# Decoder layer on one core: maxima sent to their row by transfers, softmax sums inverted on sixteen partitions, layer-norm roots in fewer operations

## The chip, the cores and the metric

The kernel runs on one NeuronCore of a Trainium2 chip. The core has a matrix engine (TensorE, PE in the profile; its weight loads are shown as PEld), a vector engine (VectorE, DVE), an engine for activation functions (ScalarE, ACT), a general engine (GpSimd, POOL) and an engine that issues transfers (SyncE, SP). Each works through its own list of instructions in a fixed order and waits on semaphores for the others. Sixteen DMA engines move data between the memory on the chip (SBUF, 128 partitions) and HBM, or from SBUF to SBUF. Matmul results land in PSUM.

The metric is the device time of one execution in microseconds. The kernel before takes 5403.67 us (median of 3 runs, 5400.97 to 5409.85).

## What is computed

A decoder layer in float32 on x of shape (8, 512, 512): a state-space block (Mamba), cross-attention to a context of the same shape, and a mixture of 32 experts, each with a residual and a layer norm. Cut to what matters here:

```
def _layernorm(x, axis=-1, eps=1e-05):
    m = jnp.mean(x, axis=axis, keepdims=True)
    v = jnp.var(x, axis=axis, keepdims=True)
    return (x - m) / jnp.sqrt(v + eps)
...
    scores = jnp.einsum('bnlh,bnph->bnlp', qm, km) / np.sqrt(HEAD_DIM).astype(np.float32)
    mask = attention_mask[:, None, None, :]
    scores = jnp.where(mask, scores, MASK_FILL)
    attn = jax.nn.softmax(scores, axis=-1)
    out = jnp.einsum('bnlp,bnph->bnlh', attn, vm)
...
    x = _layernorm(x + _L0_attn_ref(x, ...), axis=-1)
    x = _layernorm(x + _L0_xattn_ref(x, ctx_1024, ctx_1024, mask_BxS2_bf1, ...), axis=-1)
    x = _layernorm(x + _L0_ffn_ref(x, ...), axis=-1)
```

There are 16 heads of 32 dimensions, 512 queries and 512 keys in each of 8 batches.

## The kernel before, in words

`layers` handles the Mamba block, the attention and the routing; `experts` the 32 experts; `finish` the last layer norm.

The scan goes through 16 chunks (8 batches of two chunks of 256 positions). A chunk has 32 steps. In each step DVE does three large operations: the input product (L494), the scan itself (L501) and the product with C (L510); ACT makes the decays for the next step (L480); PE folds the result of two steps together (L521). Their inputs are copies of dt and dtx, four times repeated over partitions, which SP fetches with transfers (`repeat`, L428), and of B and C, which go to HBM and come back spread over the partitions (`x_proj` L408, `bcast` L418).

The attention of batch b-1 is cut into small parts by `units`, and these are laid between the steps of batch b's two chunks: a list of parts with weights, taken as the running sum allows. The attention of the last batch has no scan to lie under and runs after it. A part returns a follow-up that is put into the program a little later; `wait` puts it three thirds of a step later, and outside the scan it has no effect. The order in which each engine's instructions finally stand is fixed by the framework's scheduler when the program is built.

The parts that the change touches, for a pair of heads i (8 pairs a batch):

- `spread` (L793) brings the pair's q and k to the tiles `qa` and `ka`, 64 partitions a head: 32 rows of data, and then rows that add the mask and the negative maximum to the scores within the same matmul. The row of `qa` that will hold the maximum is first set to zero; the row of `ka` against it holds ones (L269 to L274).
- `maximum` (L805) runs four times, for 128 queries each: two matmuls (L813) with queries on the output partitions, and one DVE reduction (L815) to one value for each query and head.
- `negate` (L817) turns the 128x2 maxima into rows by four PE transposes (L822), ACT multiplies by -1 (L826), and two transfers (L829) put the rows into `qa`.
- `weigh` (L833): the matmuls the other way round (L839), keys on the partitions, and the exponential on ACT (L843).
- `gather` (L847): the product with v (L855). v has 32 columns of ones beside it, so that 32 rows of the result hold the softmax's sum. ACT copies the result to SBUF (L867), and four transfers move the products to `attT` (L875) and the sums, 32 equal rows a head, to `total` (L876).
- `divide` (L880), for two pairs of heads at a time (4 a batch, 32 in all): `total` is 128 partitions by 512 queries. Its reciprocal comes from ACT (Ln and Exp, L888 and L889) and a Newton step on DVE, and the same operations scale `attT` (L892 to L894).
- `output` (L902) is the matmul with Wo (L750), which needs all four parts of `attT`.

`layernorm` (L54) runs 40 times: ln1 and ln2 on 2 tiles in each of 16 chunks, ln3 on 4 tiles in each of 8 batches. Besides the statistics it has a DVE operation that adds EPS (L64), Ln and Exp on ACT (L68, L69) and four DVE operations (L73 to L76) that improve the root by a Newton step.

Of the kernel before, what the change touches and what calls it, by code (L numbers as in the profile page):

```python
# [17 lines left out]
P = 128  # L18
B, S, D = 8, 512, 512
DC = D // P  # L20
# [30 lines left out]
ROW = D + E + 1  # L51


def layernorm(nc, pool, tiles, outs, name, wait=lambda part: part, then=None):  # L54


    n = len(tiles)
    mv = pool.tile([P, n, 2], F32, tag=f"{name}mv")
    for j, t in enumerate(tiles):
        st = pool.tile([P, 6], F32, tag=f"{name}st")  # L60
        nc.vector.bn_stats(st, t)
        nc.vector.bn_aggr(mv[:, j, :], st)
    v = pool.tile([P, n], F32, tag=f"{name}v")
    nc.vector.tensor_scalar(v, mv[:, :, 1], EPS, None, ALU.add)  # L64

    def roots():
        r = pool.tile([P, n], F32, tag=f"{name}r")
        nc.scalar.activation(r, v, AF.Ln)  # L68
        nc.scalar.activation(r, r, AF.Exp, scale=-0.5)  # L69

        def scaled():
            m = pool.tile([P, n], F32, tag=f"{name}m")
            nc.vector.tensor_tensor(m, v, r, ALU.mult)  # L73
            nc.vector.tensor_tensor(m, m, r, ALU.mult)
            nc.vector.tensor_scalar(m, m, -0.5, 1.5, ALU.mult, ALU.add)
            nc.vector.tensor_tensor(r, r, m, ALU.mult)  # L76
            less = pool.tile([P, n], F32, tag=f"{name}less")
            nc.vector.scalar_tensor_tensor(less, mv[:, :, 0], -1.0, r, ALU.mult, ALU.mult)
            for j, (t, o) in enumerate(zip(tiles, outs)):
                nc.scalar.activation(o, t, AF.Identity, bias=less[:, j : j + 1], scale=r[:, j : j + 1])  # L80
            if then:
                then()

        return wait(scaled)

    return wait(roots)


def layers(ctx, tc, a, x1d, filld, based, xbuf):
# [38 lines left out]

    ident = cp.tile([P, P], F32, name="l_ident")
    make_identity(nc, ident)  # L130

    def const(name, shape, src):
        t = cp.tile(shape, F32, name=f"l_{name}")
# [66 lines left out]

    ones = cp.tile([P, P], F32, name="l_ones")
    nc.gpsimd.memset(ones, 1.0)
    fold = cp.tile([P, QP], F32, name="l_fold")
    for at, sign in ((0, 1), (NQ - 1, -1)):
        nc.gpsimd.affine_select(
# [57 lines left out]
    def later_constants():  # L263

        nc.sync.dma_start(
            aneg.rearrange("p c j g -> p (c j) g"),
            a["A_log"].rearrange("(b c) (s g) -> (c s) b g", c=QP, s=NQ),
        )
        for i in range(NPB):  # L269
            for r0 in (HD + 1, 2 * HD + HD + 1):  # L270
                nc.sync.dma_start(
                    kas[i][r0 : r0 + 1, :].rearrange("p (c t) -> p c t", c=DC),
                    ones[0:1, :].unsqueeze(1).to_broadcast([1, DC, P]),
                )  # L274
# [39 lines left out]
    def norm_x(f):  # L314
        xt = f["xt"]
        xs = [xt[:, j, :] for j in range(NT_)]
        return layernorm(nc, sm, xs, xs, "ln1", wait)

    def flip_x(q, f):
        if q == 0:  # L320
# [221 lines left out]
    def back(half, b, t, f):  # L542
# [15 lines left out]
        def norm():  # L558
            outs = [o[:, j, :] for j in range(NT_)]
            for j in range(NT_):  # L560
                nc.vector.scalar_tensor_tensor(outs[j], pos[j], rs, outs[j], ALU.mult, ALU.add)  # L561
            r0 = b * S + t * T
            to = x1d[r0 : r0 + T, :].rearrange("(j p) d -> p j d", p=P)
            return layernorm(nc, sm, outs, outs, "ln2", wait, lambda: nc.sync.dma_start(to, o))

        return wait(norm)

# [185 lines left out]
    def units(b):  # L753
# [51 lines left out]
        def maximum(i, lt):  # L805

            qa, ka = st[i]
            if lt == 0:
                st["mx", i] = p2.tile([P, SC, 2], F32, tag="mx", name="mx")
            ps = pss.tile([P, 2, S], F32, tag="sc", name="ps_s")  # L810
            for j in range(2):
                r = slice(j * 2 * HD, (j + 1) * 2 * HD)
                nc.tensor.matmul(ps[:, j, :], qa[r, lt * P : (lt + 1) * P], ka[r, :], start=True, stop=True)  # L813
            mx = st["mx", i]
            return lambda: nc.vector.tensor_reduce(mx[:, lt, :].unsqueeze(2), ps, AX.X, ALU.max) and None  # L815

        def negate(i):  # L817

            mx = st.pop(("mx", i))
            pm = psm.tile([P, S], F32, tag="mm", name="ps_m")  # L820
            for lt in range(SC):
                nc.tensor.transpose(pm[0:2, lt * P : (lt + 1) * P], mx[:, lt, :], ident)  # L822
# [24 lines left out]
        def gather(i, kc):  # L847
# [17 lines left out]
            def split():  # L865
                raw = p3.tile([P, D], F32, tag="row", name="raw")
                nc.scalar.copy(raw, po)  # L867
                if i % 2 == 0:
                    st["total"] = p1.tile([P, S], F32, tag="total", name="total")
                attT, total, oc = st["attT"], st["total"], i // 2  # L870
                for j in range(2):

                    r0, r1 = (0, HD) if j == 0 else (3 * HD, 2 * HD)
                    to = slice((i % 2) * 2 * HD + j * HD, (i % 2) * 2 * HD + (j + 1) * HD)
                    nc.sync.dma_start(attT[to, oc, :], raw[r0 : r0 + HD, :])  # L875
                    nc.sync.dma_start(total[to, :], raw[r1 : r1 + HD, :])  # L876

            return split

        def divide(oc):  # L880

            attT, total = st["attT"], st["total"]

            late = wait if oc < DC - 1 else lambda part: part

            def inverse():
                r = p3.tile([P, D], F32, tag="row", name="r")
                nc.scalar.activation(r, total, AF.Ln)  # L888
                nc.scalar.activation(r, r, AF.Exp, scale=-1.0)  # L889

                def newton():
                    nc.vector.tensor_tensor(total, total, r, ALU.mult)  # L892
                    nc.vector.scalar_tensor_tensor(total, total, -2.0, r, ALU.add, ALU.mult)
                    nc.vector.scalar_tensor_tensor(  # L894
                        attT[:, oc, :], attT[:, oc, :], -1.0, total, ALU.mult, ALU.mult
                    )

                return late(newton)

            return late(inverse)  # L900

        def output(lt):  # L902
# [9 lines left out]
            def add_up():  # L912
                nc.vector.tensor_tensor(xr, pp, xr, ALU.add)
                nc.vector.tensor_tensor(st["x2"][lt], xr, bo, ALU.add)
                if lt == SC - 1:
                    return layernorm(nc, sm, st["x2"], st["x2"], "ln3")

            return add_up

# [644 lines left out]
```

## Time and profile before

| | us |
|---|---|
| median of 3 runs | 5403.67 |
| the profiled execution's own time | 5406.28 |
| its span, first to last instruction | 5404.6 |
| busy in the span: PE | 4672.4 |
| DVE | 4235.9 |
| ACT | 2593.6 |
| POOL | 570.3 |
| scan with attention of batches 0 to 6 | about 503 to 3522 |
| attention of batch 7 and what follows it up to the experts | about 3522 to 3850 |
| experts | about 3850 to 5340 |

The granted TensorE clock was 0.935 over the span. In a list of groups, a line gives the source line, the engine, the operation, the tiles (out<-in), shapes and count, then the busy time in us and the mean of one in ns, and then the idle time just before these instructions and what ended it. In a list of waits: who waited for whom, total us, times, longest. In a timeline: start, duration, engine and line; in brackets the idle time before it and its releaser. A letter q after an engine's name means its sequencer; SPq lines are issues of transfers, not their duration.

### The profile page before, as it was taken

To read this page: it belongs to the slowest core of one execution; us is meant where nothing else is said; L and a number is where in the kernel's file an instruction comes from. 1 tells how busy PE (TensorE), PEld (TensorE's weight loads), DVE (VectorE), ACT (ScalarE), POOL (GpSimd) and SP (SyncE) were. 2 spreads that over 40 slices of the span, in tenths; PEclk is the share of its full clock that TensorE was granted. 3 is DMA by queue.
4 is the path that set the end of the run, shared out by engine and by line. 5 is a ranking of instruction groups with operands and counts; after the bars stand their busy time and mean duration, and the time that the engine had idled before them with its cause. 6 is when DMAs were issued, how large, how long until landed. Compare 5 with 4: busy or idle time off the path is not lost. (4 is left out here: it accounts for less than half of the span.)

```text
span 5404.6 us, 53991 instructions
## 1 busy us (share of the span) xinstructions
PE 4672.4 (86%) x17320; PEld 2476.6 (46%) x17320; DVE 4235.9 (78%) x5369; ACT 2593.6 (48%) x5726; POOL 570.3 (11%) x426
## 2 busy tenths in 40 slices
PE   6768889788888988988888888789999999999994
PEld 3324234234333423433333342333677777777773
DVE  7999899989989989898998998943566555665554
ACT  5566565565656556566565655523222222222223
POOL 1000002002000200200200020011111111111111
PEclk8879989999999999999999999899999999999997
DMA  8875346345444634634544463342344444544544
GB/s 236 266 224 146 87 96 208 81 114 176 114 104 117 197 77 109 189 98 107 174 125 100 117 200 78 91 146 66 103 128 127 123 117 118 127 127 121 129 115 144
DMA packets 486427, 719.03 MB, mean 133 GB/s; under 512 B 117137, under 2 KB 200625, under 8 KB 484096
## 3 DMA queue, kind: packets, MB, share of 16 engines
q1 hardware_dynamic: 450128, 627.16, 41.1%
q0 software_dynamic: 33280, 76.90, 7.5%
q10 hardware_dynamic: 2736, 11.54, 0.5%
q8 instruction: 137, 2.24, 0.2%
q14 instruction: 146, 1.20, 0.1%
HBM read 391.24 MB, written 165.05 MB: 103 GB/s over the span
## 5 line engine op out<-in xcount | busy, mean ns | idle before, releaser
L480 ACT ACTIVATE l_da<-rep,l_aneg 128x256 f32<-128x256 f32 x2048 | 895.0, 501 | 941.8 <-DVE h L501 877.0
L501 DVE TENSOR_TENSOR_SCAN h<-l_da,h 128x1028 f32<-128x1028 f32 x512 | 1166.0, 2292 | 20.3 <-ACT l_da L480 17.7
L494 DVE TENSOR_TENSOR h<-rep,bc 128x1024 f32<-128x1024 f32 x512 | 614.7, 1218 | 103.1 <-PE py L521 84.6
L510 DVE TENSOR_TENSOR h<-h,bc 128x1024 f32<-128x1024 f32 x512 | 619.5, 1217 | 2.1
L521 PE MATMUL py<-h,l_fold 128*32 128x512 f32 x2048 | 368.3, 644 | 113.4 <-DVE h L510 96.5
L813 PE MATMUL ps_s<-l_ka,l_qa 64*128 64x512 f32 x1024 | 325.6, 707 | 137.8 <-DVE mx L815 137.6
L1314 PE MATMUL ps_h<-xT,w 128*128 128x320 f32 x1536 | 435.8, 433 | 0.0
L1394 POOL DMA_INDIRECT based<-y,xe x160 | 255.5, 1597 | 1309.9 <-ACT y L1417 630.0
L1335 DVE TENSOR_TENSOR hT<-ps_h,p 128x320 f32<-128x320 f32 x128 | 62.9, 492 | 378.5 <-PE ps_h L1314 378.5
L815 DVE TENSOR_REDUCE mx<-ps_s 128x2 f32<-128x1024 f32 x256 | 310.2, 1217 | 58.5 <-PE ps_s L813 58.3
L1314 PEld LDWEIGHTS ps_h<-xT,w 128*128 128x128 f32 x1536 | 292.5, 191 | 118.3 <-issue 0.4
L855 PE MATMUL po<-eT,l_va 128*64 128x512 f32 x1024 | 301.5, 670 | 47.6 <-ACT eT L843 43.1
L839 PE MATMUL ps_t<-l_qa,l_ka 64*128 64x512 f32 x1024 | 308.4, 674 | 23.8 <-ACT eT L843 23.1
L843 ACT ACTIVATE eT<-ps_t 128x1024 f32<-128x1024 f32 x256 | 259.0, 1015 | 128.8 <-PE ps_t L839 128.5
L688 POOL DMA_INDIRECT xbuf<-x2t,dest x128 | 217.2, 1697 | 860.4 <-DVE dest L679 760.8
L1314 PE MATMUL ps_h<-t,s 128*128 128x320 f32 x1024 | 286.1, 432 | 0.0
L343 PE MATMUL ps_z<-xnT,wm 128*128 128x256 f32 x1024 | 238.0, 388 | 30.0 <-DVE o L561 24.3
L750 PE MATMUL ps_p<-x2T,wa 128*128 128x512 f32 x512 | 241.5, 626 | 18.1 <-ACT hT L944 10.4
L552 PE MATMUL po<-wm,zs 128*128 128x512 f32 x512 | 244.7, 632 | 13.8 <-DVE z L957 11.9
L343 PE MATMUL ps_x<-xnT,wm 128*128 128x256 f32 x1024 | 246.5, 393 | 4.5 <-ACT xnT L332 2.5
L343 PEld LDWEIGHTS ps_z<-xnT,wm 128*128 128x128 f32 x1024 | 194.6, 193 | 93.0 <-DVE o L561 37.5
L343 PEld LDWEIGHTS ps_x<-xnT,wm 128*128 128x128 f32 x1024 | 196.1, 195 | 80.5 <-issue 43.8
(232 smaller groups left out, 7170.4 us busy)
## 6 DMA issues: line engine op xcount, KB each, us to landing
w<-in_w SPq DMA_DIRECT2D x93, 1024.0 KB
wm<-in_in_proj_w SPq DMA_DIRECT2D x128, 512.0 KB
rep<-dt SPq DMA_DIRECT2D x256, 256.0 KB
rep<-dtx SPq DMA_DIRECT2D x256, 256.0 KB
xbuf<-zero SPq DMA_DIRECT2D x32, 1362.5 KB
xe<-xbuf SPq DMA_DIRECT2D x32, 1362.5 KB
wm<-in_out_proj_w SPq DMA_DIRECT2D x64, 512.0 KB
wa<-in_sw SPq DMA_DIRECT2D x24, 1024.0 KB
```

Source lines behind the costliest of these rows:

```text
L343: nc.tensor.matmul(ps[:, i, :], w[:, dc, i * P : (i + 1) * P], f["xnT"][:, dc, :], start=(dc == 0), stop=(dc == DC - 1),)
L480: nc.scalar.activation(da[:, n, 1:], dt[:, j, i, :], AF.Exp, scale=aneg[:, 2 * q + i, 2 * jj + j, g : g + 1])
L494: nc.vector.tensor_tensor(h[:, :, 1:], dtx.rearrange("p j i t -> p (j i) t"), f["bc", g][0], ALU.mult)
L501: nc.vector.tensor_tensor_scan(flat, da.rearrange("p n t -> p (n t)"), flat, 0.0, ALU.mult, ALU.add)
L510: nc.vector.tensor_tensor(h[:, :, 0:T], h[:, :, 1:], f["bc", g][1], ALU.mult)
L521: nc.tensor.matmul(f["py"][j * QP : (j + 1) * QP, :, :], fold, hs[j // 2][:, 2 * (j % 2) : 2 * (j % 2) + 2, 0:T], start=False, stop=g == N ...
L813: nc.tensor.matmul(ps[:, j, :], qa[r, lt * P : (lt + 1) * P], ka[r, :], start=True, stop=True)
L815: return lambda: nc.vector.tensor_reduce(mx[:, lt, :].unsqueeze(2), ps, AX.X, ALU.max) and None
L839: nc.tensor.matmul(ps[:, j, :], ka[r, kc * P : (kc + 1) * P], qa[r, :], start=True, stop=True)
L843: nc.scalar.activation(eT, ps, AF.Exp)
L855: nc.tensor.matmul(po[j * 2 * HD : (j + 1) * 2 * HD, :], va[:, kc, i, j * HD : (j + 2) * HD], eT[:, j, :], start=(kc == 0), stop=(kc == SC ...
L1314: nc.tensor.matmul(ps, w[:, n, r * P : (r + 1) * P], x[:, n, :], start=not more and n == 0, stop=n == 1, skip_group_check=more,)
```

## The change

Three things are changed.

The maxima are kept so that one partition's four values lie together, and the queries are dealt out so that partition p holds the queries 4p to 4p+3. For that the weights of L813 are read with a step of four elements. Then the 128x4 values of a head are already in the order of the row, and one transfer a head sends them there. The sign moves into the constant row of `ka`, which becomes -1. The transposes, the multiplication on ACT and their PSUM slot go. The new part has weight 0 instead of 0.4.

Of each head's 32 equal rows of sums, one goes to four partitions of a 16x128 tile. After two pairs, DVE takes the reciprocal there (the instruction of that name), one transfer writes the 16x128 values to HBM, another reads them back to 128 partitions, each head's 512 values 32 times. One DVE multiplication scales `attT`. Ln, Exp and the Newton step go.

In `layernorm` EPS becomes the bias of ACT's Ln, and the Newton step is put into three operations with two ALU steps each.

```diff
-    v = pool.tile([P, n], F32, tag=f"{name}v")
-    nc.vector.tensor_scalar(v, mv[:, :, 1], EPS, None, ALU.add)
+    v = mv[:, :, 1]
...
-        nc.scalar.activation(r, v, AF.Ln)
+        nc.scalar.activation(r, v, AF.Ln, bias=eps)
...
-            nc.vector.tensor_tensor(m, v, r, ALU.mult)
-            nc.vector.tensor_tensor(m, m, r, ALU.mult)
-            nc.vector.tensor_scalar(m, m, -0.5, 1.5, ALU.mult, ALU.add)
-            nc.vector.tensor_tensor(r, r, m, ALU.mult)
+            nc.vector.scalar_tensor_tensor(m, v, EPS, r, ALU.add, ALU.mult)
+            nc.vector.scalar_tensor_tensor(m, m, -0.5, r, ALU.mult, ALU.mult)
+            nc.vector.scalar_tensor_tensor(r, m, 1.5, r, ALU.add, ALU.mult)
...
+    minus = cp.tile([1, P], F32, name="l_minus")
+    nc.gpsimd.memset(minus, -1.0)
...
-                    ones[0:1, :].unsqueeze(1).to_broadcast([1, DC, P]),
+                    minus.unsqueeze(1).to_broadcast([1, DC, P]),
...
-                st["mx", i] = p2.tile([P, SC, 2], F32, tag="mx", name="mx")
+                st["mx", i] = p2.tile([P, 2, SC], F32, tag="mx", name="mx")
...
-                nc.tensor.matmul(ps[:, j, :], qa[r, lt * P : (lt + 1) * P], ka[r, :], start=True, stop=True)
+                own = qa[r, :].rearrange("k (p l) -> k l p", l=SC)[:, lt, :]
+                nc.tensor.matmul(ps[:, j, :], own, ka[r, :], start=True, stop=True)
...
-        def negate(i):
+        def subtract(i):
 
             mx = st.pop(("mx", i))
-            pm = psm.tile([P, S], F32, tag="mm", name="ps_m")
-            for lt in range(SC):
-                nc.tensor.transpose(pm[0:2, lt * P : (lt + 1) * P], mx[:, lt, :], ident)
-
-            def put():
-                nm = p3.tile([P, D], F32, tag="row", name="nm")
-                nc.scalar.mul(nm[0:2, :], pm[0:2, :], -1.0)
-                for j in range(2):
-                    r0 = j * 2 * HD + HD + 1
-                    nc.sync.dma_start(st[i][0][r0 : r0 + 1, :], nm[j : j + 1, :])
-
-            return put
+            for j in range(2):
+                r0 = j * 2 * HD + HD + 1
+                nc.sync.dma_start(st[i][0][r0 : r0 + 1, :], mx[:, j, :])
...
-                    st["total"] = p1.tile([P, S], F32, tag="total", name="total")
+                    st["total"] = p1.tile([4 * SC, P], F32, tag="few", name="few")
...
-                    nc.sync.dma_start(total[to, :], raw[r1 : r1 + HD, :])
+                    h0 = (i % 2) * 2 + j
+                    nc.sync.dma_start(few[h0 * SC : (h0 + 1) * SC, :], raw[r1 : r1 + 1, :])
...
-                r = p3.tile([P, D], F32, tag="row", name="r")
-                nc.scalar.activation(r, total, AF.Ln)
-                nc.scalar.activation(r, r, AF.Exp, scale=-1.0)
-
-                def newton():
-                    nc.vector.tensor_tensor(total, total, r, ALU.mult)
-                    nc.vector.scalar_tensor_tensor(total, total, -2.0, r, ALU.add, ALU.mult)
-                    nc.vector.scalar_tensor_tensor(
-                        attT[:, oc, :], attT[:, oc, :], -1.0, total, ALU.mult, ALU.mult
-                    )
-
-                return late(newton)
+                nc.vector.reciprocal(few, few)
+                flat = dp.tile([4, S], F32, tag="flat", name="flat")
+                nc.sync.dma_start(flat.rearrange("h (s t) -> (h s) t", s=SC), few)
+                total = p1.tile([P, S], F32, tag="total", name="total")
+                nc.sync.dma_start(total, flat.unsqueeze(1).to_broadcast([4, HD, S]))
+
+                def scaled():
+                    nc.vector.tensor_tensor(attT[:, oc, :], attT[:, oc, :], total, ALU.mult)
+
+                return late(scaled)
...
-                add(0.4, negate, late.pop(), dry=True)
+                add(0, subtract, late.pop(), dry=True)
```

More of the change, by code (lines that the diff above doesn't have):

```diff
@@ L51, with layernorm @@
 ROW = D + E + 1
-def layernorm(nc, pool, tiles, outs, name, wait=lambda part: part, then=None):
+def layernorm(nc, pool, tiles, outs, name, eps, wait=lambda part: part, then=None):
     n = len(tiles)
@@ L130, in layers @@
     make_identity(nc, ident)
+    eps = cp.tile([P, 1], F32, name="l_eps")
+    nc.gpsimd.memset(eps, EPS)
     def const(name, shape, src):
@@ L316, in norm_x @@
         xs = [xt[:, j, :] for j in range(NT_)]
-        return layernorm(nc, sm, xs, xs, "ln1", wait)
+        return layernorm(nc, sm, xs, xs, "ln1", eps, wait)
     def flip_x(q, f):
@@ L563, in norm @@
             to = x1d[r0 : r0 + T, :].rearrange("(j p) d -> p j d", p=P)
-            return layernorm(nc, sm, outs, outs, "ln2", wait, lambda: nc.sync.dma_start(to, o))
+            return layernorm(nc, sm, outs, outs, "ln2", eps, wait, lambda: nc.sync.dma_start(to, o))
         return wait(norm)
@@ L812, in maximum @@
                 r = slice(j * 2 * HD, (j + 1) * 2 * HD)
-                nc.tensor.matmul(ps[:, j, :], qa[r, lt * P : (lt + 1) * P], ka[r, :], start=True, stop=True)
+                own = qa[r, :].rearrange("k (p l) -> k l p", l=SC)[:, lt, :]
+                nc.tensor.matmul(ps[:, j, :], own, ka[r, :], start=True, stop=True)
             mx = st["mx", i]
-            return lambda: nc.vector.tensor_reduce(mx[:, lt, :].unsqueeze(2), ps, AX.X, ALU.max) and None
-        def negate(i):
+            return lambda: nc.vector.tensor_reduce(mx[:, :, lt].unsqueeze(2), ps, AX.X, ALU.max) and None
+        def subtract(i):
             mx = st.pop(("mx", i))
-            pm = psm.tile([P, S], F32, tag="mm", name="ps_m")
-            for lt in range(SC):
-                nc.tensor.transpose(pm[0:2, lt * P : (lt + 1) * P], mx[:, lt, :], ident)
-            def put():
-                nm = p3.tile([P, D], F32, tag="row", name="nm")
-                nc.scalar.mul(nm[0:2, :], pm[0:2, :], -1.0)
-                for j in range(2):
-                    r0 = j * 2 * HD + HD + 1
-                    nc.sync.dma_start(st[i][0][r0 : r0 + 1, :], nm[j : j + 1, :])
-            return put
+            for j in range(2):
+                r0 = j * 2 * HD + HD + 1
+                nc.sync.dma_start(st[i][0][r0 : r0 + 1, :], mx[:, j, :])
         def weigh(i, kc):
@@ L868, in split @@
                 if i % 2 == 0:
-                    st["total"] = p1.tile([P, S], F32, tag="total", name="total")
-                attT, total, oc = st["attT"], st["total"], i // 2
+                    st["total"] = p1.tile([4 * SC, P], F32, tag="few", name="few")
+                attT, few, oc = st["attT"], st["total"], i // 2
                 for j in range(2):
@@ L875, in split @@
                     nc.sync.dma_start(attT[to, oc, :], raw[r0 : r0 + HD, :])
-                    nc.sync.dma_start(total[to, :], raw[r1 : r1 + HD, :])
+                    h0 = (i % 2) * 2 + j
+                    nc.sync.dma_start(few[h0 * SC : (h0 + 1) * SC, :], raw[r1 : r1 + 1, :])
             return split
         def divide(oc):
-            attT, total = st["attT"], st["total"]
+            attT, few = st["attT"], st["total"]
             late = wait if oc < DC - 1 else lambda part: part
             def inverse():
-                r = p3.tile([P, D], F32, tag="row", name="r")
-                nc.scalar.activation(r, total, AF.Ln)
-                nc.scalar.activation(r, r, AF.Exp, scale=-1.0)
-                def newton():
-                    nc.vector.tensor_tensor(total, total, r, ALU.mult)
-                    nc.vector.scalar_tensor_tensor(total, total, -2.0, r, ALU.add, ALU.mult)
-                    nc.vector.scalar_tensor_tensor(
-                        attT[:, oc, :], attT[:, oc, :], -1.0, total, ALU.mult, ALU.mult
-                    )
-                return late(newton)
+                nc.vector.reciprocal(few, few)
[6 more added lines that the diff above has]
+                return late(scaled)
             return late(inverse)
@@ L915, in add_up @@
                 if lt == SC - 1:
-                    return layernorm(nc, sm, st["x2"], st["x2"], "ln3")
+                    return layernorm(nc, sm, st["x2"], st["x2"], "ln3", eps)
             return add_up
```

## The prediction

> **What bounds the kernel now.** The chain that ended last covers only about the final 100 us (the expert output and the last layer norm), which the change leaves alone. So I read by stage: the busy time of each engine in stretches, then the waits of each engine inside the stage, then single stretches of the timeline. All sums are in microseconds of the profiled execution: span 5404.6, that run 5406.28, median of the three runs 5403.67.
>
> ```profile
> core 0: us, PE busy (x) PEld busy (x) DVE busy (x) ACT busy (x) POOL busy (x), PEclk, DMA share, GB/s
> 503.00:3522.00 3019.00, 2544.14 (x9192) 1081.90 (x9190) 2747.18 (x2977) 1777.18 (x3940) 250.24 (x177) 0.93 0.47 125
> 3601.00:3704.00 103.00, 101.75 (x419) 30.70 (x420) 45.05 (x41) 45.25 (x55) 0.14 (x1) 1.00 0.17 42
> ```
>
> The first row is the seven attention batches that run inside the scan (503 to 3522 us): VectorE (DVE) is busy 91%, TensorE (PE) 84%, ScalarE (ACT) 59%. DVE sets the pace there, and PE is not far behind. The second row is the eighth attention batch, after the scan has ended: PE is busy 99%, DVE 44%. From about 3850 us the experts run, untouched. The waits in the first stage:
>
> ```profile
> DVE h L494 <- PE py L521: 84.6, 35, 5.4
> DVE mx L815 <- PE ps_s L813: 14.0, 17, 1.4
> PE ps_s L813 <- DVE mx L815: 137.1, 94, 4.2
> PE ps_m L822 <- DVE mx L815: 74.9, 35, 3.4
> ACT l_da L480 <- DMA rep<-dt: 46.9, 31, 5.0
> ```
>
> (total, times, longest.) DVE's 272 us of idle time there is mostly waiting for PE and ACT; PE in turn stands still 74.9 us ahead of the transposes that the change removes, because they need the last maximum.
>
> **Part 1, DVE work that goes.** The rows, with the mean of one in ns after the comma:
>
> ```profile
> L892 DVE TENSOR_TENSOR total<-total,r 128x512 f32<-128x512 f32 x32 | 21.8, 681 | 22.4 <-ACT r L889 22.1
> L893 DVE SCALAR_TENSOR_TENSOR total<-total,r 128x512 f32<-128x512 f32 x32 | 21.9, 684 | 0.6
> L894 DVE SCALAR_TENSOR_TENSOR attT<-attT,total 128x512 f32<-128x512 f32 x32 | 22.0, 688 | 0.6
> L64 DVE TENSOR_SCALAR v<-mv 128x2 f32<-128x2 f32 x32 | 5.4, 168 | 0.8
> L78 DVE SCALAR_TENSOR_TENSOR less<-mv,r 128x2 f32<-128x2 f32 x32 | 5.1, 159 | 1.0
> L640 DVE RECIPROCAL g_ws<-g_ws 128x4 f32<-128x4 f32 x8 | 1.4, 170 | 0.0
> ```
>
> One divide now costs 681 + 684 + 688 = 2053 ns. Afterwards: one multiply (681) and a reciprocal of 16x128. No row has that; it lies between 170 ns (L640, 4 elements a partition) and 681 ns (512 elements). Rows with 128 elements a partition are nearest (L636 227 ns, L642 293 ns), so 250. Saved 1.12 us, bounds 0.69 to 1.20; 28 of the 32 divides lie in the DVE-bound stage: 31 us (19 to 34). A layer norm has five operations for L64 and L73 to L76, 817 ns on two columns, 805 on four; afterwards three at the L78 row (159; 142 on four columns): 0.34 and 0.38 us less. In the stage: 15 ln1 and 15 ln2 at 0.34 and 7 ln3 at 0.38, 13 us. **Together -44 us.** What ACT loses (Ln and Exp, 0.62 us each, and 0.58 us for L826) lies under a busier DVE: I count it at nothing. If ACT were the bound it would be a gain.
>
> **Part 2, maxima straight to their row.** Gone are 224 transposes in the stage (41.3 us of PE, from the busy time of L822 in it), the 74.9 us that PE waits there, a PSUM slot for each pair of heads, and ACT's L826. DVE does not get this one for one: PE's other wait for the same reduction (L813, 137 us) takes up much of what is freed. DVE's own waits on PE that could shrink are 84.6 + 14.0. **I take -10**, bounds 0 and -75.
>
> The two transfers of a pair stay two on SP's queue, but now wait for the reduction instead of ACT. Behind them on SP stand the copies of dt and dtx (L428) that ACT and DVE need. Before, SP was released at L829 by ACT 124.1 us in the stage; now by the last reduction, earlier by two steps. The rows are written as 128 pieces of 16 bytes; the queue gives no row for such a transfer, but the first pair of the last batch shows the room: its reduction ends by 3606.9, the transfers go at 3608.0. That 1.1 us is what the landing may be slower. Later pairs have two rounds of PE work (2.9 to 3.0 us each: L813 starts at 3642.57, 3645.55 and 3648.48) before the row is read, and the old transfer was waited for 0.3 us in all. Counted at nothing.
>
> The weights of L813 are now read with a step of four elements. Nothing in the trace reads weights so. Below: no cost. Above: the load's part that grows with columns, 186 ns (L813) less 82 ns (L822, two columns), comes twice: 104 ns on each of 1024 loads. Most of a load lies under a running matmul (four loads take 0.30 us together), so in the DVE-bound stage I take nothing, and in the PE-bound batch 3 us of at most 13 (128 loads).
>
> The Trainium skill (SBUF — State Buffer, "Door 1: The DMA port swizzle") speaks against this: it says that SBUF is read in lines of 16 bytes and every access that goes to a new line pays. Each weight element is then on its own line; it gives no price, and with loads twice as long and unhidden the sum would end 10 us higher.
>
> **Part 3, the sums over HBM.** Now: total lands, then Ln, Exp, three DVE operations. The tail of the last batch, with nothing else running:
>
> ```profile
> 3706.06 0.59 SPq L876 DMA_DIRECT2D total<-raw  x1
> 3708.27 0.63 ACT L888 ACTIVATE r<-total 128x512 f32<-128x512 f32 x1 [4.06 <-DMA total<-raw]
> 3709.59 0.69 DVE L892 TENSOR_TENSOR total<-total,r 128x512 f32<-128x512 f32 x1 [16.22 <-ACT r L889]
> 3711.80 10.55 PE L750 MATMUL ps_p<-wa,attT 128*128 128x512 f32 x20 [3.72 <-DVE attT L894]
> ```
>
> From the end of the issue to the landing 1.6 us, from there 3.5 us to the end of L894; PE stands still for it. Afterwards: landing 1.6, reciprocal 0.25, to HBM, spread, multiply 0.7. To HBM: between 1.9 (0.33 issue and the same 1.6) and 3.3, which is what the like step of the scan takes at the start:
>
> ```profile
> 40.30 0.33 SPq L408 DMA_DIRECT2D scr<-xd  x1
> 43.62 0.64 SPq L418 DMA_DIRECT2D bc<-scr  x1
> ```
>
> Spread of 256 KB: between 2.0 (L428's last dtx copy: issue ends 59.30, L494 starts 60.67, and 0.6 of issue) and 7.0 (twice the bytes: the out_proj weights issued at 3557.79 release PE at 3564.82). I take 2.6 and 3.0: 8.2 instead of 5.1, **+3 in the tail**, once.
>
> In the scan DVE need not stand still: the order put Ln 2.3 to 4 us or more after the transfers and DVE only waited for it once (2.3 us). What matters is how late the spread lands against its place in DVE's fixed order; behind the multiply stand the scan's own three operations, and ACT's decays wait for those. Nearest row: the dt copies, also 256 KB, stop ACT 46.9 us for 112 pairs of copies, 0.42 each. Two transfers in a row: 0.84, times 28, **+23**. Bounds: 0.06 (dtx copies stop DVE 6.5 us for 112) and 5.0 (the longest stop): 2 to 140. SP gets two more issues a divide, 64 x 0.6 = 38 us of its time in the whole run, and stands behind the first landing (at L418 this is 1.1 us a time); I take nothing, since the wait at L829 shortens by as much.
>
> The Trainium skill (DMA: Bandwidth & Descriptors, "Rules for kernel authors") has a rule against this spread: a transfer whose outermost dimension has c entries under 16 stays on c engines. The source here is 4 x 32 x 512. By the page's 27 GiB/s for an engine, an estimate, 64 KB on each of four take 2.3 us instead of 0.6; if DVE waited for all of that, 28 x 1.7 = 48 us would come on top and the forecast would be 5422. No run yet shows a transfer on four engines.
>
> **Sum.** -44 - 10 + 23, and the last batch: transposes -4 (0.53 us, L822 at 3639.11 to L813 at 3639.64, times 8), last divide +3, weights +3, two exposed layer norms -1: +1. In all -30: span 5375, median **5374**.
>
> **Rivals.** (a) Slower: the spread is late at the multiply. One mechanism: DVE stops in each of 28 divides. Without this term the sum is -53, so it decides from 1.9 us a divide; at 3.5 us, +98 - 53 = +45: 5449. For: two landings in a row, 4.2 us at the least. Against: DVE has hardly waited for transfers so far. (b) No change: DVE's freed time returns as waiting for PE, 84% busy: about 5400. For: 84.6 us of such waits already. Against: PE is relieved by 41 us too. (c) Slower by the strided weights: 93 us of longer loads on PE in the stage, 13 in the last batch; if half of the former reaches DVE, -30 + 46 + 10: 5430. Against: loads are hidden. (d) The row arrives later than before, though sent earlier: L839 would wait for it; the room above speaks against it, and I give it no share of its own.
>
> **Chances.** Forecast 0.54 (its own range 5335 to 5392), (b) 0.13, (a) 0.25, (c) 0.08. Faster by over 0.2% (11 us, what a measurement can just tell) 0.54, same 0.13, slower 0.33. Below, 5330 takes in a larger relief of PE (-55 instead of -10); above, 5435 takes in (c) and half of (a).
>
> **What would show it.** DVE busy in the stage down by about 44 and its idle time no higher than 300; no line of DVE waiting for the spread over 30 us in all; no PE wait for the transposes; L813's loads still near 186 ns; the last batch as long as before. I am wrong if DVE's wait ahead of the new multiply is 1.9 us or more on average, or if L813's loads grow and DVE's waits on ps_s with them.

## The result and the profile after

The changed kernel takes 5460.66 us (median of 4 runs, 5457.57 to 5467.47), against 5403.88 for the kernel before beside it: ratio 1.0107 [1.0093, 1.012], slower by 57 us where 30 less had been forecast. The profiled span is 5455.9 us, 51.3 more than before. The scan ends at 3557 us instead of 3522; from the first maximum of the last batch to the first expert matmul it is 3634.5 to 3848.5, 214 us instead of 200 (3600.9 to 3800.8). So 35 us are lost in the scan, some 13 between its end and the experts, and a few elsewhere.

The stretches of the kernel after that answer to the two shown of before (the scan with seven attention batches, and 103 us from the last batch's first maximum on):

```profile
503.00:3557.00 3054.00, 2576.48 (x8950) 1121.67 (x8949) 2725.04 (x2879) 1749.94 (x3839) 166.38 (x177) 0.92 0.45 124
3634.00:3737.00 103.00, 95.63 (x354) 35.20 (x356) 47.51 (x45) 31.58 (x35) 0.00 (x0) 0.95 0.15 39
```

DVE's busy time in the scan fell from 2747.2 to 2725.0, half of the 44 us forecast, and its idle time rose from 272 to 329 us. In the last batch PE is no longer busy throughout: 95.6 of 103 us instead of 101.8. From its first maximum to the first expert matmul PE waits 6.2 us more at L816 for the reductions and 4.2 more for the last divide. The granted TensorE clock in the scan is 0.92 against 0.93; run 5 below has 0.93 like the kernel before, and its scan ends 30 us later all the same, so the clock alone does not make the difference. What DVE waits for in the scan (total us, times, longest), kernel after:

```profile
DVE h L496 <- PE py L523: 78.2, 48, 4.5
DVE h L496 <- DMA rep<-dtx: 34.9, 10, 5.9
...
DVE mx L818 <- PE ps_s L816: 24.7, 38, 1.3
DVE attT L889 <- DMA l_qa<-qT: 23.7, 4, 6.0
...
DVE attT L889 <- DMA l_qa<-l_ka: 11.7, 2, 5.9
DVE attT L889 <- DMA total<-flat: 10.4, 3, 6.3
DVE few L882 <- DMA few<-raw: 9.0, 8, 1.8
```

Two things are new. The multiplication at L889 waits for transfers; it reads nothing of `l_qa`, so the rows that name it are the same wait put down to another transfer of the queue. Summed over the 28 divides of the scan, DVE stands 58.6 us ahead of L889 (2.1 us a divide) and 9.0 ahead of the reciprocal: 2.4 us a divide together. And the scan's input product (L496) waits 34.9 us for the copies of dtx, where it waited 6.5. The wait for PE's py is no longer than before (84.6).

The groups that the prediction priced (busy us, mean ns of one, then idle time ahead), kernel after:

```profile
L882 DVE RECIPROCAL few<-few 16x128 f32<-16x128 f32 x32 | 29.8, 931 | 24.4 <-DMA few<-raw 24.4
L889 DVE TENSOR_TENSOR attT<-attT,total 128x512 f32<-128x512 f32 x32 | 21.9, 685 | 77.5 <-DMA l_qa<-qT 30.0 <-DMA total<-flat 22.9 <-DMA l_qa<-l_ka 11.7
```

The reciprocal was taken as 0.25 us and takes 0.93. The last divide with nothing else running, kernel after (start, duration):

```profile
3748.58 0.61 SPq L871 DMA_DIRECT2D few<-raw  x1
3750.47 0.94 DVE L882 RECIPROCAL few<-few 16x128 f32<-16x128 f32 x1 [9.82 <-DMA few<-raw]
3751.43 0.31 SPq L884 DMA_DIRECT2D flat<-few  x1
3752.78 0.56 SPq L886 DMA_DIRECT2D total<-flat  x1
3757.82 0.69 DVE L889 TENSOR_TENSOR attT<-attT,total 128x512 f32<-128x512 f32 x1 [6.41 <-DMA total<-flat]
```

From the end of the last issue of `few` (3749.19) to the end of the multiplication 9.3 us, forecast 8.2, before 5.1. The sums reach HBM in 1.4 us (2.6 forecast); the spread takes 5.0 us from its issue to the multiplication (3.0 forecast).

### The profile page after: what moved, and what is told of

Same layout as the page of the kernel before. It is cut to its first block, busy times and chain, and to the rows that moved or that the text cites. A ratio compares the mean times of both kernels' runs of the same rounds, so it can differ in the third digit from the quotient of the medians.

```text
span 5455.9 us, 53341 instructions
## 1 busy us (share of the span) xinstructions
PE 4714.7 (86%) x17064; PEld 2524.5 (46%) x17064; DVE 4212.0 (77%) x5257; ACT 2561.9 (47%) x5617; POOL 487.8 (9%) x428
## 5 line engine op out<-in xcount | busy, mean ns | idle before, releaser
L496 DVE TENSOR_TENSOR h<-rep,bc 128x1024 f32<-128x1024 f32 x512 | 613.0, 1216 | 132.5 <-PE py L523 78.2
L816 PE MATMUL ps_s<-l_ka,l_qa 64*128 64x512 f32 x1024 | 349.8, 762 | 206.7 <-DVE mx L818 202.0
L523 PE MATMUL py<-h,l_fold 128*32 128x512 f32 x2048 | 400.6, 665 | 95.4 <-DVE h L512 90.7
L816 PEld LDWEIGHTS ps_s<-l_ka,l_qa 64*128 64x128 f32 x1024 | 144.0, 316 | 418.7 <-DVE mx L818 325.2
L833 PE MATMUL ps_t<-l_qa,l_ka 64*128 64x512 f32 x1024 | 305.8, 675 | 26.5 <-ACT eT L837 13.6
```

What stands on the lines that cost most here:

```text
L496: nc.vector.tensor_tensor(h[:, :, 1:], dtx.rearrange("p j i t -> p (j i) t"), f["bc", g][0], ALU.mult)
L523: nc.tensor.matmul(f["py"][j * QP : (j + 1) * QP, :, :], fold, hs[j // 2][:, 2 * (j % 2) : 2 * (j % 2) + 2, 0:T], start=False, stop=g == N ...
L816: nc.tensor.matmul(ps[:, j, :], own, ka[r, :], start=True, stop=True)
L833: nc.tensor.matmul(ps[:, j, :], ka[r, kc * P : (kc + 1) * P], qa[r, :], start=True, stop=True)
```

## The experiments

The first four runs set theory A, that the sums over HBM are what costs, against B, that the maxima are. The texts of the later runs name further ones. N: the spread lies on few DMA engines, lands late, and DVE stops for it; against it M, that two landings in a row are late on however many engines. O: the change gives the scheduler another program, and the order in which it now lays the instructions costs time whatever the operations are. P: each added operation has its own price (strided weights, reciprocal, transfers on SP's queue). Q: what SP issues holds up the copies of dt and dtx behind it. R stands for the rival that its text describes. Every run below is timed in five rounds beside the kernel before; "alone" means one part of the change laid on the kernel before.

| run | median us | ratio to before, 95% |
|---|---|---|
| 1 layer norms alone | 5371.53 | 0.9949 [0.9934, 0.9963] |
| 2 divide over HBM alone | 5505.62 | 1.0189 [1.0175, 1.0202] |
| 3 maxima part alone | 5436.36 | 1.0064 [1.0049, 1.0078] |
| 4 strided weights alone | 5410.77 | 1.0015 [1.0007, 1.0024] |
| 5 run 2, spread on 16 engines | 5443.29 | 1.0070 [1.0054, 1.0086] |
| 6 run 5, sums on 128 partitions | 5455.09 | 1.0094 [1.0079, 1.0109] |
| 7 run 3, transfers by GpSimd | 5435.43 | 1.0055 [1.0043, 1.0067] |
| 8 layer norms + 6 + 7 | 5429.93 | 1.0045 [1.0032, 1.0058] |
| 9 weight 0 alone | 5436.99 | 1.0064 [1.0051, 1.0077] |
| 10 maxima part, weight 0.4 | 5394.66 | 0.9978 [0.9968, 0.9988] |
| 11 run 5, transfers by GpSimd | 5447.85 | 1.0077 [1.0064, 1.0089] |
| 12 run 2, nobody waits for the spread | 5391.44 | 0.9982 [0.9974, 0.9991] |
| 13 whole change, weight 0.4 | 5441.51 | 1.0065 [1.0051, 1.0079] |
| 14 layer norms + 10 | 5370.55 | 0.9936 [0.9922, 0.9949] |
| 15 run 13, spread on 16 engines | 5381.11 | 0.9950 [0.9936, 0.9964] |
| 16 Newton step in three operations alone | 5405.28 | 1.0001 [0.9993, 1.0010] |
| 17 run 15, sums on 128 partitions | 5375.97 | 0.9952 [0.9940, 0.9965] |
| 18 EPS as bias alone | 5408.85 | 1.0013 [1.0005, 1.0022] |

**Each part alone (1 to 3).** The edits are the three parts of the diff shown above.

> The kernel before with the layer norms alone changed. Both theories: two small DVE operations fewer in each of 40 norms, 13 us less DVE work in the scan; time 8 to 16 us under before (about 5391). If it is not faster, DVE's busy time is not what sets the pace and the first step of the prediction falls too.

> The kernel before with the divide alone changed. Theory A (the sums over HBM are what costs: the spread lands late and holds DVE at the multiply, and the reciprocal takes 0.93 us): 45 to 60 us over before (5449 to 5464), DVE waiting over 55 us in the scan ahead of the multiply, and hardly less DVE work. Theory B (the maxima cost; DVE's stops at the multiply only take the place of other waits): within 15 us of before.

> The kernel before with the maxima alone changed (strided weights, rows sent by transfers, no transposes). Theory A: within 12 us of before, either way. Theory B (weights read with a step load 120 ns longer each, and SP stands at the reductions with the dt copies behind it): 40 to 65 us over before, with more waiting for the dt and dtx copies.

Alone the parts are worth -31, +103 and +34 us; together +57. All three lie outside the ranges expected: the layer norms gain twice as much, the divide loses twice as much as A had it, and the maxima lie between A and B. The parts do not add, so more counts than what each does by itself.

**Strided weights alone (4).** The transposes stay; ACT writes the maxima back in the order of the row.

```diff
-                nc.tensor.matmul(ps[:, j, :], qa[r, lt * P : (lt + 1) * P], ka[r, :], start=True, stop=True)
+                own = qa[r, :].rearrange("k (p l) -> k l p", l=SC)[:, lt, :]
+                nc.tensor.matmul(ps[:, j, :], own, ka[r, :], start=True, stop=True)
```

> The kernel before, transposes and all, with only the weights of the maxima's matmuls read with a step of four elements (ACT writes the negative maxima back in the order of the row). It prices the strided loads by themselves: they should take 306 instead of 186 ns. Theory A: 3 to 15 us over before, of it 4 us in the last batch (32 maxima by 0.12 us). Theory B: 30 us or more over before.

The loads of weights in run 4, one line of the kernel (count, then shortest, median and longest in ns):

```profile
L814 PEld LDWEIGHTS ps_s<-l_ka,l_qa x1024: 304/306/328, 502.9 to 3689.5; 64*128 64x128 f32 x171
```

The kernel before has a median of 186 ns there. So the loads do grow, by 120 ns. That agrees with the 16-byte rule of the Trainium skill (SBUF — State Buffer, "Door 1: The DMA port swizzle"); no other step was tried, so no run shows that the lines are the reason. The whole costs 8 us in the median, as A had it: the scan ends where it did (3523 us), and from there to the first expert matmul it is 283 us instead of 279, about what 32 rounds of PE in the last batch at 0.12 come to.

**The spread on sixteen engines (5).** The four heads of a divide are dealt out over the partitions in turn, and rows of Wo and bv are permuted to match. The spread's outermost dimension then has 32 entries instead of 4. Bytes, instructions and their order on each engine are those of run 2.

```diff
-                    to = slice((i % 2) * 2 * HD + j * HD, (i % 2) * 2 * HD + (j + 1) * HD)
+                    to = slice((i % 2) * 2 + j, P, 4)
...
-                nc.sync.dma_start(total, flat.unsqueeze(1).to_broadcast([4, HD, S]))
+                nc.sync.dma_start(total, flat.unsqueeze(0).to_broadcast([HD, 4, S]))
```

> As e2_spread_only, with the heads interleaved over the partitions (partition 4d+h instead of 32h+d, rows of Wo and bv laid out to match), so that the spread reads 32 x 4 x 512 instead of 4 x 32 x 512. The engines' instructions stand in the same order as in e2. Theory N (the spread runs on four DMA engines, and this makes it late): it lands 2 us or less after its issue instead of about 5.4, DVE's wait ahead of the multiply in the scan falls from 96 to 25 us or less, time 5410 to 5440. Theory M (two landings in a row and SP's stand between them make it late, on however many engines): landing over 4 us, the wait stays over 70 us, time over 5480.

The last divide's spread and multiplication, first run 2, then run 5 (the line of the issue on SP, the line of DVE):

```profile
3814.28 0.58 SPq L892 DMA_DIRECT2D total<-flat  x1
...
3819.32 0.69 DVE L895 TENSOR_TENSOR attT<-attT,total 128x512 f32<-128x512 f32 x1 [6.42 <-DMA total<-flat]
```

```profile
3740.47 0.56 SPq L892 DMA_DIRECT2D total<-flat  x1
...
3743.61 0.69 DVE L895 TENSOR_TENSOR attT<-attT,total 128x512 f32<-128x512 f32 x1 [4.51 <-DMA total<-flat]
```

From the end of the issue 4.5 us against 2.6. The stretch in which this spread moves its bytes, again run 2, then run 5 (columns as at the start; the last but one is the mean busy share of the 16 DMA engines):

```profile
3815.64:3818.64 3.00, 0.00 (x0) 0.00 (x0) 0.00 (x0) 0.00 (x0) 0.00 (x0) 0.64 0.23 87
```

```profile
3741.82:3743.05 1.23, 0.00 (x0) 0.00 (x0) 0.00 (x0) 0.00 (x0) 0.00 (x0) 0.50 0.69 212
```

0.23 of sixteen is 3.7 engines' work, 0.69 is 11. In the scan DVE's stops at L895 fall from 95.8 to 40.2 us, and the time by 62 us. M falls. The mechanism is theory N's, and the rule of the Trainium skill (DMA: Bandwidth & Descriptors, "Rules for kernel authors"), with nothing changed but the outermost dimension; the sizes fell short of N's (25 us of stops or less, 5410 to 5440). Most of the stops that are left are some 5 us at each batch's first divide, and the run is still 37 us slower than the kernel before.

**Nobody waits for the spread (12).** Run 2 with all its transfers; the multiplication reads a constant tile, so the softmax's sums are left out of the output.

> The divide over HBM alone as in the change (four entries in the spread's outermost dimension, 5506), with every transfer and the reciprocal still issued, but the multiplication reads a constant tile instead of what the spread brings: the softmax's sums are left out of the output, and nobody waits for the spread. Theory N (the late landing at the multiply is the largest cost): its 96 us of DVE's stops go and the time falls by 60 to 100 us, to 5405 to 5445. Theory R (the transfers, the reciprocal and the order cost it, the stop at the multiply would be replaced by others): 5470 or more.

114 us less than run 2, more than N's 60 to 100, and 13 less than the kernel before. So the reciprocal and the transfers by themselves cost nothing that shows. But the run takes away more than the wait: the multiplication no longer depends on a transfer, and the scheduler laid the instructions in another order. The first two steps of a batch, which take 9.6 us in the kernel before and 25.0 in run 2, take 9.6 again (the seam described at run 9). So the 114 us are those of the late landing and of the order together, and this run can't part them.

**The sums on 128 partitions (6), and whose queue (7, 11).** Run 6 lays the sums on 128x16 before the reciprocal. Run 7 gives the transfers of the maxima to GpSimd, run 11 the write to HBM and the spread.

```diff
-                    st["total"] = p1.tile([4 * SC, P], F32, tag="few", name="few")
+                    st["total"] = p1.tile([P, S // HD], F32, tag="few", name="few")
...
-                nc.sync.dma_start(st[i][0][r0 : r0 + 1, :], mx[:, j, :])
+                nc.gpsimd.dma_start(st[i][0][r0 : r0 + 1, :], mx[:, j, :])
```

> As e5_spread_wide, with the sums before the reciprocal on 128 partitions by 16 instead of 16 by 128. If the reciprocal's 0.93 us comes from its 128 elements a partition, it takes about 0.25 us here, DVE is busy 19 us less in the scan, and the time is 10 to 20 us under e5. If it comes from something else, it stays at 0.93 and the time is that of e5.

> As e3_max_only, with the two transfers of the maxima issued by GpSimd instead of SP. PE's and DVE's instructions stand nearly in the same order as in e3. Theory Q (SP stands at the last reduction, and the dt and dtx copies behind it come late): waits for the dtx copies in the scan fall from 40 to about 10 us and for the dt copies from 70 to 50 or less; time 5400 to 5415, the price of the strided loads being left. Theory O (the other order of the instructions and PE's longer loads are the cause): still over 5428, with DVE's waits for PE (112 us) as they were.

> The divide over HBM with the spread on sixteen engines (5443), its write to HBM and its spread now issued by GpSimd instead of SP; PE's and DVE's order is nearly the same. Theory Q (these issues stand on SP ahead of the copies of dt and dtx and make them late): ACT's waits for the dt copies fall from 116 us to under 70, and the time to 5405 to 5425. Theory R (the copies are late because of the order or the DMA engines, not because of SP): waits over 90 us, time 5433 to 5453.

The reciprocal falls to 244 ns in run 6, yet the time rises by 12 us, which neither reading had; why stays open. Moving the transfers off SP changes nothing in either case: 5435 against 5436, and 5448 against 5443, with ACT still waiting 113.6 us for the copies of dt (run 5: 115.9). SP's queue is not the cause. Nor do those waits by themselves make a run slow: in run 15 below they are 135.3 us, and it is fast.

**All repairs known then (8).**

> The whole change with the spread on 16 engines, the reciprocal on 128 partitions and the maxima's transfers on GpSimd's queue. If the prices found so far are all, it gives back the 57 us and lands under before: 5360 to 5390. If it stays over 5404, something else in the change costs.

5430: still slower than before, while the layer norms alone give 5372. The cause of the maxima part's loss was not yet among the repairs. And although the spread lies on sixteen engines here, DVE stands 57 us ahead of the multiplication in the scan: in six of the seven batches the order has put one instruction only between the third divide's reciprocal and its multiplication, where the changed kernel has nine, and DVE stops 6 to 7 us there. How much a late landing costs is a matter of the order too.

**One number (9, 10).** The change also gives the part that follows the last maximum the weight 0 instead of 0.4. `units` lays the parts of a batch between the scan's steps by the running sum of these weights; eight parts with 0.4 less move all the parts behind them. Run 9 is the kernel before with that number alone, run 10 the maxima part with the old number.

```diff
-                add(0.4, negate, late.pop(), dry=True)
+                add(0, negate, late.pop(), dry=True)
```

> The kernel before with one number changed: the part that turns the maxima into a row has weight 0 instead of 0.4, as the change has it. No instruction is added, removed or altered; their order on every engine is different. Theory O (the order alone is worth tens of us, and most of the maxima part's 34 us is this): a time more than 12 us away from the kernel before, either side, likeliest slower, 5415 to 5435, with DVE's waits for py and dtx up as in the maxima part alone (py 84.6 to about 110). Theory P (the operations of the maxima part have their price, the order costs nothing): within 8 us of the kernel before.

> The kernel before with the maxima part alone, the weight of its last piece kept at 0.4 instead of 0. The operations are those of the maxima part alone (5436), their order is another. Theory O: at least 12 us away from 5436, and with an order nearer to that of the kernel before 5400 to 5420. Theory P: 5428 to 5444.

The number alone costs 33 us, as much as the whole maxima part; with the number kept, that part is 9.5 us faster than the kernel before (5394.7, where O had 5400 to 5420). Theory O, and the rival P falls. Where the time goes is seen in the waits of DVE in the scan of run 9:

```profile
DVE h L494 <- PE py L521: 108.5, 55, 5.5
DVE dtx L457 <- ACT dtx L453: 50.7, 13, 4.9
DVE h L494 <- DMA rep<-dtx: 42.1, 10, 5.4
```

Before, these were 84.6, 28.5 and 6.5 us. The place is the seam between two batches. The kernel before, timeline of DVE at one seam: the end of the preparation of dtx, and the first input products of the next batch:

```profile
2186.28 0.69 DVE L460 TENSOR_TENSOR dtx<-dt,xs 128x512 f32<-128x512 f32 x1
...
2199.27 2.35 DVE L494 TENSOR_TENSOR h<-rep,bc 128x1024 f32<-128x1024 f32 x2
```

The same in run 9:

```profile
2203.62 0.69 DVE L460 TENSOR_TENSOR dtx<-dt,xs 128x512 f32<-128x512 f32 x1
...
2211.54 2.36 DVE L494 TENSOR_TENSOR h<-rep,bc 128x1024 f32<-128x1024 f32 x2 [4.46 <-DMA rep<-dtx]
2221.76 1.23 DVE L494 TENSOR_TENSOR h<-rep,bc 128x1024 f32<-128x1024 f32 x1 [5.05 <-DMA rep<-dtx]
```

Before, dtx was ready 12.3 us ahead of its use, with 22 other DVE instructions between, and the copies had landed. In run 9 nine stand between; dtx is ready 7.2 us ahead, of which DVE stands 4.5, and it stops a second time. By the ends of the scan instructions (mean of the last six batches) the first two steps of a batch take 25.3 us instead of 9.6; some of it comes back in later steps. In run 10 they take 9.6 again. In the changed kernel they take 24.6, and its timeline shows the same seam:

```profile
2212.34 0.68 DVE L462 TENSOR_TENSOR dtx<-dt,xs 128x512 f32<-128x512 f32 x1
...
2218.37 2.36 DVE L496 TENSOR_TENSOR h<-rep,bc 128x1024 f32<-128x1024 f32 x2 [2.43 <-DMA rep<-dtx]
...
2226.49 1.23 DVE L496 TENSOR_TENSOR h<-rep,bc 128x1024 f32<-128x1024 f32 x1 [2.95 <-DMA rep<-dtx]
```

Counted so in the traces of all runs ("between": the other DVE instructions between that dtx operation and the batch's first input product; the two steps as a mean of the last six batches):

| runs | between | first two steps, us |
|---|---|---|
| before, 4, 10, 12, 16, 18 | 22 | 9.6 |
| 1, 14 | 21 | 10.8 |
| 13, 15, 17 | 11 | 14.2 to 14.3 |
| 2, 5, 6, 11 | 17 | 24.6 to 25.1 |
| changed kernel, 3, 7, 8, 9 | 9 | 24.1 to 25.3 |

So the divide alone (2, 5, 6, 11) makes the seam late as well, at the old weight: the weight is one way to such an order, not the only one. In run 9 the order also gives ACT 7 more loads of function tables (132 for 125, 9 us in all; the changed kernel has 144); their share of the 33 us was not parted from that of the seam.

**Do these two causes account for the change (13, 15)?** The changed kernel with the weight 0.4, and the same with the spread on sixteen engines, where the order of the instructions on each engine is the same.

> The changed kernel with one number put back: weight 0.4 for the part that sends the maxima to their row. If the weight's cost (42 us between the two forms of the maxima part alone) is there in the changed kernel too: 5410 to 5435. If what slows it is the spread alone and the order is as good or bad by chance: within 15 us of 5461, either side.

> As the run before last (the changed kernel with weight 0.4), and the heads dealt out so that the spread goes over sixteen engines, the instructions' order the same. If the late spread is what is left of the loss: 40 to 65 us less than the changed kernel with weight 0.4, 5355 to 5390. If not: within 15 us of it.

The weight is worth 19 us here (5460.7 to 5441.5), less than the 42 between runs 3 and 10; the time lies in neither of the two ranges. The four-engine spread is worth 60 (5441.5 to 5381.1), as expected. The two are not prices that stand by themselves: with the spread on sixteen engines already, the weight is worth 54 (run 8, 5429.9, to run 17 below, 5376.0, which differ also in the queue of the maxima's transfers); and DVE's stops ahead of L889, with four entries, are 58.6 us at weight 0 and 79.3 at 0.4 (run 13). The scan of run 13, then of run 15 (columns as at the start):

```profile
503.00:3550.00 3047.00, 2567.12 (x8950) 1121.13 (x8949) 2730.53 (x2883) 1721.68 (x3828) 248.79 (x177) 0.92 0.46 124
```

```profile
503.00:3497.00 2994.00, 2559.36 (x8953) 1119.24 (x8952) 2728.45 (x2883) 1725.45 (x3829) 241.18 (x177) 0.93 0.46 126
```

DVE's work is the same to 2 us; the 53 us by which the scan is shorter are idle time, and DVE's stops ahead of L889 in it fall from 79 to 27. With both repaired, what the change set out to do is 24.5 us faster than the kernel before.

**The reciprocal again (17), and the layer norms (14, 16, 18).** Run 16 keeps EPS as an operation of DVE and shortens the Newton step; run 18 makes EPS the bias of the logarithm and keeps four operations of the Newton step.

> The changed kernel with weight 0.4, the spread on sixteen engines, and the sums before the reciprocal on 128 partitions x 16 instead of 16 x 128. If the reciprocal's 0.68 us more than predicted is paid for on DVE's path: 15 to 25 us less than with it on 16 partitions (5381), 5355 to 5368. If it lies in the time that DVE waits anyway, or the many small pieces of the transfers take it back: 5375 to 5395.

> The kernel before with the layer norms and the maxima part at weight 0.4; the divide is the old one. If the parts' gains add (-31 and -9): 5358 to 5372, the fastest yet. If the gain of the layer norms was the luck of one order and its work is worth 13 us: 5378 to 5395.

> The kernel before with the layer norms' Newton step in three operations, EPS still added by an operation of DVE: four operations instead of five in each layer norm. By the work removed on DVE (about 0.17 us each of 37 in the scan, 6 us): 5394 to 5401. If any shorter chain between the statistics and the norm brings the larger gain: 5370 to 5390.

> The kernel before with EPS as the bias of the logarithm alone; the Newton step keeps its four operations, the first of which adds EPS. DVE has one operation less in a layer norm, as in the run before, but here it stands between the statistics and the logarithm. If the gain of the layer norms lies in that shorter step to ACT: 5370 to 5390. If the removed work of DVE is all: 5396 to 5404; if only both halves together give an order that brings the gain, within 8 us of the kernel before.

Run 17's reciprocal in the groups:

```profile
L882 DVE RECIPROCAL few<-few 128x16 f32<-128x16 f32 x32 | 7.8, 244 | 22.8 <-DMA few<-raw 21.8 <-DMA l_qa<-mx 1.0
```

DVE's busy time in the scan falls by 15 us against run 15 (2728.5 to 2713.6), and the scan ends at the same 3497 us; the times can't be told apart (intervals overlap). Work taken from DVE became waiting here. The layer norms show the opposite. The scan of run 1:

```profile
503.00:3483.00 2980.00, 2553.35 (x9190) 1082.87 (x9190) 2737.64 (x2911) 1779.24 (x3938) 246.89 (x177) 0.94 0.47 127
```

DVE is busy 9.5 us less than before, but the scan is 39 us shorter: its idle time fell by 29. Yet neither half alone gives any of it (5405 and 5409). Run 14's 5370.6 lies in what adding the gains would give, but it can't be told from the layer norms alone (5371.5), so the maxima part added nothing there. Both beat the kernel before and the changed one; nothing tried was faster. Why the layer norms need both halves stays open: that another order is behind it, as in run 9, is only argued.

## Why the prediction was wrong

The forecast was -30, the result +57. The rival that came true is (a), the late spread, and beside it stands a cause that the prediction did not have. That (a)'s 5449 is near is partly luck: it was for 3.5 us a divide, the runs show 2.1 to 2.4, and the weight added to it.

| step of the prediction | forecast us | what the runs show |
|---|---|---|
| Part 1, DVE's work in the scan | -44 | -22 of busy time: the divide -12 for -31, the layer norms -9.5 for -13 |
| Part 2, maxima (relief -10, transposes -4, weights +3) | -11 | -9.5 with weight 0.4 (run 10) |
| weight 0 for 0.4 | no term | +33 alone (run 9), +19 in the whole change (13), 54 with the spread on sixteen engines (8 to 17) |
| Part 3, late spread in the scan | +23 | 67.6 us of DVE's stops in the changed kernel; the four entries alone +60 (13 to 15), with 29 us of stops still left |
| last divide | +3 | +4 (9.3 us for 5.1) |
| last batch in all (some of it in the rows above) | +1 | +14 (214 us for 200) |

**The step that failed** is in Part 3: "Nearest row: the dt copies, also 256 KB, stop ACT 46.9 us for 112 pairs of copies, 0.42 each. Two transfers in a row: 0.84, times 28". The row was of the right size in bytes but of another kind: those copies have 32 entries in their outermost dimension (QP at L428), not four. The prediction had the rule on four engines, worked out 1.7 us a divide from it, and put it aside because no run showed it. The runs show some 2 us: 60 us over 28 divides. The rival's own bound, "it decides from 1.9 us a divide", was met by 2.1 us of DVE's stops ahead of the multiplication. The stop came at each batch's first divide (about 6 us), where three DVE instructions stand between the reciprocal and the multiplication, and at the fourth (2 to 3); the ones between found more work ahead of the multiplication.

**What was not in the sum** is the weight. The text of the change named it, and no step priced it. It is a number of the planner, not an instruction, so no row of the trace has a price for it; what the trace could have told is that dtx stood ready 12.3 us ahead at a seam. Where DVE waits for the copies (run 13, the changed kernel), its use comes 5 to 8 us behind dtx, so some 4 to 7 us were to spare, an estimate.

**Sizes.** The reciprocal, 0.25 taken and 0.93 measured: rows with 128 elements a partition were taken as like it, though none was a reciprocal; L640, which is one, had four. It cost DVE 19 us of work in the scan, but run 17, in the order of run 15 but for a few places, shows 15 us of them off the path. So the -44 was wrong by half, and its being whole would not by itself have brought the time down: DVE's busy share of 91% was not the bound that the sum took it for. Rival (b), freed time that returns as waiting, had that mechanism, though the waiting in run 17 is not for PE alone.

**What held.** The strided loads are hidden in the scan, though their price was 120 ns, above the bound of 104. The sign that was set for rival (c) did come, longer loads and DVE's waits on ps_s (14.0 us before, 24.7 after); but with the strided loads alone those waits are 13.2 us and the scan ends at 3523 us, so (c) fell. The maxima part was sized rightly at the old weight, though not in its parts: in run 10 DVE's idle time in the scan fell by 6 us (272 to 266), and its wait for PE's py, which was to shrink, grew (84.6 to 105.9). The row of maxima is not late (no wait of L833 is put down to its transfer), and PE's wait for the transposes is gone; of PE's relief much was taken up by its wait for the reduction (137.1 us before, 195.3 after), as said. The forecast without the spread's term was -53; run 15, which still has 29 us of stops for the divide's transfers in the scan, is at -24.5. That -53 and 29 make -24 is partly luck, for the layer norms gave more than their term and the relief of DVE less.

## What to carry to other kernels

Look at the outermost dimension of every transfer that something waits for; if it has few entries, as the four here, try more (here 32), even if tiles have to be permuted for that. In a kernel whose order is laid by weights, a weight is part of the change: try it alone, and keep it when operations change. An experiment that takes a wait away can change the order too: compare the orders before its gain is put down to the wait. Price a stall by how far ahead of its use a thing is ready at the tightest place (here the seam between two batches and each batch's first divide), not by an engine's busy share: 15 us of DVE work removed brought nothing in run 17, while the order of run 9, with its stops of 3 to 5 us at the seams, cost 33 us.

## What the runs showed of the hardware

- A spread of 256 KB from HBM to 128 partitions: 4.5 us from the end of its issue to the start of its reader with four entries outermost, 2.6 with 32 (last divide, quiet queues); in the scan 5.4 to 6.8 us in the changed kernel. While it moves, the 16 DMA engines are busy 0.23 of the time with four entries, 0.69 with 32.
- DVE's reciprocal: 931 ns for 128 elements a partition on 16 partitions, 244 ns for 16 elements on 128; from these two an estimate of about 6 ns for each further element. A multiplication of 512 elements takes 685.
- Loading 64x128 weights with a step of four elements: 306 ns instead of 186.
- The sums written to HBM in pieces of 64 bytes from 128 partitions (run 17) come back as soon as in pieces of 512 bytes from 16 (run 15): from the reciprocal's end to the multiplication 4.8 us against 4.7 in the last divide.
